# Newton's step of the inverse roots moved to GpSimd, with new places and issue lengths in the plan of the FFN steps

## The chip, the core and the metric

The kernel runs on one core of a Trainium2 chip. The core has five engines with an instruction stream each: TensorE (PE in the profile; its weight loads are shown as PEld), VectorE (DVE), ScalarE (ACT), GpSimd (POOL) and SyncE (SP), which here only issues transfers. Each engine works through its own stream in order and waits at semaphores for the others. The metric is the device time of one execution in microseconds. Every number on the profile comes from one profiled execution.

## The reference

The input is x of shape (8, 512, 128), in float32. Three parts follow one another, each with a residual:

```python
x = x + 0.5 * ffn(layernorm(x))
x = x + latent_attention(layernorm(x))      # 16 heads, causal
x = x + 0.5 * ffn(layernorm(x))             # the same weights as the first

def layer(x):                               # ffn: two of these
    q, k, v = split(shift_token(x) @ wqkv)  # 8 heads of 64
    q = l2norm(q) * q_scale; k = l2norm(k) * k_scale
    q, k = rotary_xpos(q, k)
    p = softmax(mask(8 * q @ k.T))          # windows of 64, each with the one before it
    x = x + (p @ v) @ wo
    h = shift_token(x)
    h = (h - mean(h)) / sqrt(var(h) + 1e-5) * ln_g + ln_b
    a, g = split(h @ w1 + b1)               # 341 columns each
    return x + (a * gelu(g)) @ w2 + b2
```

`shift_token` takes the second half of the 128 channels from the token before. `l2norm` divides each head's 64 values by their norm. So inverse roots are needed in two places: one per token for each layer norm, and one per token, head and side (q or k) for `l2norm`.

## The kernel before

The program has three stages: the FFN part (called f0), the latent attention, and the FFN part again (f1). The FFN stages take two passes (layers) over eight sequences of 512 tokens, so 16 sequences per stage, each in four blocks of 128 tokens. All of X and of the running result Y stays in SBUF.

**Steps.** The function `ffn` doesn't write its instructions directly. It makes *steps* (`step`, line 412): a kind, an engine, a length in us that the plan believes, what is read and written, which buffers are taken, and a function that issues the instructions. The kinds that matter here, with their engine:

- A sequence begins with a norm in the first layer (ist on DVE: statistics; inr on ACT: first guess of the root; ina on DVE: apply), then sh (PE: transposes), sd, sp and sa, which build the shifted transpose hT.
- A block begins with projections qk0, qk1 and v (PE). From each of q and k ACT makes the squares (sq), DVE the two rotary products (cs, lines 543 and 546), and POOL adds them (ad, line 562). ACT copies v out of PSUM (vc), and SP copies it, shifted by 64 tokens, into V2 with two transfers (vd and ve, lines 574 and 580).
- rn (DVE, lines 586 and 589) sums the squares per head. ir (ACT, lines 466 and 467) makes the first guess of the inverse root as exp(-0.5 ln x). nt (DVE, lines 470 to 472) refines it by one step of Newton. km (POOL, line 598) multiplies k by it, and q8 (POOL, line 607) makes 8 times q's root, the scale of the scores.
- tq and tc turn q and k (PE, ACT). sc (PE) makes the scores; mx (DVE, lines 669 and 670) the maxima times q8; ex (ACT, line 677) the exponentials with their sums; rc (DVE) the reciprocals; dv (POOL, line 685) the division. pt (PE) and pc (DVE or ACT, line 723) turn the probabilities; o (PE, line 743) multiplies them with V and V2, oc (ACT) copies, wo (PE) projects, and ya (DVE, line 775) adds into Y.
- After the fourth block the feed-forward part follows: hs (POOL, line 785) copies the unshifted half of Y; hd and he (SP, lines 791 and 798) bring in the other half, shifted by one partition, by transfers. hd covers 127 partitions, he the tokens at the blocks' edges. Then fst (DVE, lines 482 to 484), fnr (ACT) and fna (DVE) normalise in place; b2 (POOL, line 809) adds the bias to Y, which it may only do once hd and he have read Y. Then ft, fc, g, ge, a, u, po (the two products with the gate, line 831 and line 873), y2 and, in the second layer, fi (both DVE) follow. In f1 a transfer fo (SP, line 900) writes the result.

The refinement itself is in `root` (line 462), which returns two functions: `first` for ACT and `newton` for DVE. In the norms `newton` is called at the head of the step "na"; for l2norm it is the step "nt" by itself. An inverse root is refined for 16 numbers per partition in nt and for 4 in a norm. The latent attention has its own `inverse_root` (line 369).

**The plan.** A step's rank is `100 * at + PLACE[kind]` (line 413), where `at` is the number of its block over the whole stage; steps of the start and of the feed-forward part have the number of the sequence's first block. `Plan.run` (line 161) sorts the steps by rank and then plays the stage through: among the first 110 steps still to do (`AHEAD`) it looks which can start when (`ready`, line 122), given the lengths, the buffers, and 0.2 us for a signal between engines. It takes the engine that can begin first and on it the step of lowest rank that can begin within `WHILE` of that time. So PLACE is both a priority on each engine and a limit on how early a step is seen. A step's last number, `after`, is added before others may use its result; for a transfer it stands for the time until it has landed. The order that comes out is fixed in the program: each engine, SP's queue included, runs its instructions in it. The plan's lengths set only the order; on the chip every instruction takes as long as it takes and waits for what it needs.

Of the kernel before, what the change touches and what calls it, by code (L numbers as in the profile page):

```python
# [11 lines left out]
ALU = mybir.AluOpType  # L12
# [8 lines left out]
class PartPool:  # L21
# [7 lines left out]


PLACE = {
    "ist": -350, "inr": -670, "ina": -499, "sh": -750, "sd": -770, "sp": -690, "sa": -560,
    "qk0": -460, "sq0": -600, "cs0": -290, "ad0": -300, "qk1": -350, "sq1": -420, "cs1": -400,
    "ad1": -420, "v": -319, "vc": -89, "vd": -69, "ve": -29, "rn": -118, "ir": -48, "nt": -238,
    "km": -98, "q8": -407, "tq0": -250, "tc0": -600, "tq1": -169, "tc1": -29, "sc": -40,
    "mx": 100, "ex0": 230, "rc0": 90, "dv0": 370, "ex1": 171, "rc1": 131, "dv1": 271, "pt0": 150,
    "pc0": 230, "pt1": -809, "pc1": -909, "o": 190, "oc": 330, "wo": 0, "ya": 70, "hs": 100,
    "hd": 950, "he": 990, "fst": 830, "fnr": 180, "fna": 321, "b2": 500, "ft": 540, "fc": 690,
    "g": 1050, "ge": 1260, "a": 581, "u": 871, "po": 520, "y2": 940, "fi": 790, "fo": 1270,
}  # L40


# [41 lines left out]
class Plan:  # L84
# [5 lines left out]

    SIGNAL = 0.2
    AHEAD = 110
    WHILE = 0.05

    def __init__(self, tc, nc):
        self.tc, self.nc = tc, nc
# [92 lines left out]
def kernel(  # L189
# [219 lines left out]
    def ffn(tagname, last):  # L409
# [52 lines left out]
        def root(x, y, t):  # L462


            def first():
                nc.scalar.activation(y.tile, x.tile, AF.Ln)  # L466
                nc.scalar.activation(y.tile, y.tile, AF.Exp, scale=-0.5)  # L467

            def newton():
                nc.vector.scalar_tensor_tensor(t.tile, y.tile, -0.5, y.tile, ALU.mult, ALU.mult)  # L470
                nc.vector.tensor_mul(t.tile, t.tile, x.tile)
                nc.vector.scalar_tensor_tensor(y.tile, t.tile, 1.5, y.tile, ALU.add, ALU.mult)

            return first, newton

        def norm(k, w, src, dst, reads, writes, slots):

            st, mv, rs, ns, nt = (Slot(r) for r in (r_st, r_mv, r_rs, r_ns, r_nt))

            def stats():  # L480
                for i in range(NB):
                    nc.vector.bn_stats(st[:, i], src()[:, i])
                    nc.vector.bn_aggr(mv[:, i], st[:, i])
                nc.vector.tensor_scalar(rs.tile, mv[:, :, 1], LN_EPS, None, ALU.add)

            first, newton = root(rs, ns, nt)

            def apply():
                newton()
                for i in range(NB):  # L490
                    nc.vector.tensor_scalar(
                        dst()[:, i], src()[:, i], mv[:, i, 0:1], ns[:, i : i + 1],
                        ALU.subtract, ALU.mult,
                    )

            step(w + "st", DVE, 1.6, k, stats, reads, [rs], [st, mv, rs] + slots)
            step(w + "nr", ACT, 0.45, k, first, [rs], [ns], [rs, ns])
            step(w + "na", DVE, 1.7, k, apply, [ns] + reads, writes, [mv, rs, ns, nt] + slots)

        def transposes(src, dst):  # L500
            for i in range(NB):
# [25 lines left out]
        def begin(l, b, i, k):  # L527
            hT, kT, V2, V = seqs[l, b]
            sq, qk = Slot(r_sq), Slot(r_qk)
            x, y, t, q8 = (Slot(r) for r in (r_sums, r_root, r_half, r_q8))  # L530

            def project(ps, at):
                nc.tensor.matmul(  # L533
                    ps.tile, lhsT=hT[:, i * P : (i + 1) * P],
                    rhs=wqkv_sb[l][:, at * INNER : (at + 1) * INNER], start=True, stop=True,
                )

            for s in range(2):
                ps, c1, s1 = Slot(mm), Slot(r_c), Slot(r_s)

                def turned(s=s, ps=ps, c1=c1, s1=s1):
                    psv = ps.tile.rearrange("p (h d) -> p h d", d=DH)
                    nc.vector.tensor_mul(  # L543
                        c1.tile, psv, tabs[l][:, 2 * s, i].unsqueeze(1).to_broadcast([P, H, DH])
                    )
                    nc.vector.tensor_mul(  # L546
                        s1.tile.rearrange("p h (t d) -> p h t d", t=2),
                        psv.rearrange("p h (t d) -> p h t d", t=2)[:, :, ::-1],
                        tabs[l][:, 2 * s + 1, i].rearrange("p (t d) -> p t d", t=2)
                        .unsqueeze(1).to_broadcast([P, H, 2, HD]),  # L550
                    )

                step(f"qk{s}", PE, 0.91, k, lambda s=s, ps=ps: project(ps, s), [hT], [ps], [ps, hT], 0.1)
                step(
                    f"sq{s}", ACT, 0.5, k,
                    lambda s=s, ps=ps: nc.scalar.activation(sq[:, s], ps.tile, AF.Square),  # L556
                    [ps], [sq], [ps, sq], 0.1,
                )
                step(f"cs{s}", DVE, 1.25, k, turned, [ps], [c1], [ps, c1, s1], 0.1)
                step(  # L560
                    f"ad{s}", POOL, 1.28, k,
                    lambda s=s, c1=c1, s1=s1: nc.gpsimd.tensor_add(  # L562
                        qk[:, s].rearrange("p (h d) -> p h d", d=DH), c1.tile, s1.tile
                    ),
                    [c1], [(qk, s)], [c1, s1, qk],
                )
            ps = Slot(mm)
            step("v", PE, 0.95, k, lambda: project(ps, 2), [hT], [ps], [ps, hT], 0.1)
            step(
                "vc", ACT, 0.5, k, lambda: nc.scalar.copy(V[:, i], ps.tile),  # L570
                [ps], [(V, i)], [ps, V], 0.1,
            )
            step(
                "vd", SP, 0.1, k, lambda: nc.sync.dma_start(out=V2[WIN:, i], in_=V[:WIN, i]),
                [(V, i)], [(V2, i)], [V, V2], 3.0,
            )
            if i + 1 < NB:
                step(
                    "ve", SP, 0.1, k,
                    lambda: nc.sync.dma_start(out=V2[:WIN, i + 1], in_=V[WIN:, i]),  # L580
                    [(V, i)], [(V2, i + 1)], [V, V2], 3.0,
                )


            def sums():
                nc.vector.tensor_reduce(
                    x.tile, sq.tile.rearrange("p s (h d) -> p (s h) d", d=DH), AX.X, ALU.add
                )
                nc.vector.tensor_scalar(x.tile, x.tile, 1e-24, None, ALU.max)

            first, newton = root(x, y, t)
            step("rn", DVE, 1.3, k, sums, [sq], [x], [sq, x])
            step("ir", ACT, 0.45, k, first, [x], [y], [x, y])
            step("nt", DVE, 0.55, k, newton, [x, y], [(y, 1)], [x, y, t])

            def scale_k():
                kv = qk[:, 1].rearrange("p (h d) -> p h d", d=DH)
                nc.gpsimd.tensor_mul(  # L598
                    kv, kv, y[:, H:].unsqueeze(2).to_broadcast([P, H, DH])
                )  # L600

            step(
                "km", POOL, 1.05, k, scale_k, [(y, 1), (qk, 1)], [(qk, 2)], [y, qk],
            )
            step(
                "q8", POOL, 0.25, k,
                lambda: nc.gpsimd.tensor_scalar(q8.tile, y[:, :H], 8.0, None, ALU.mult),
                [(y, 1)], [q8], [y, q8],
            )
            blk[l, b, i] = qk, q8  # L610
# [168 lines left out]
        def feed_forward(l, b, k):  # L779
# [4 lines left out]
            def near():  # L784
# [2 lines left out]

            step("hs", POOL, 0.6, k, near, y, [(hs, 0)], [hs])
            step(
                "hd", SP, 0.1, k,  # L790
                lambda: nc.sync.dma_start(
                    out=hs[1:P, :, half:], in_=Y[0 : P - 1, b, :, half:]
                ),
                y, [(hs, 1)], [hs], 3.0,
            )
            step(
                "he", SP, 0.1, k,
                lambda: nc.sync.dma_start(
                    out=hs[0:1, 1:NB, half:], in_=Y[P - 1 : P, b, 0 : NB - 1, half:]
                ),  # L800
                y, [(hs, 2)], [hs], 3.0,
            )
            norm(
                k, "f", lambda: hs, lambda: hs, [(hs, 0), (hs, 1), (hs, 2)], [(hs, 3)], [hs]
# [84 lines left out]
            if l == L - 1:  # L889
                step(  # L890
                    "fi", DVE, 0.65, k,
                    lambda: nc.vector.scalar_tensor_tensor(
                        res.tile if last else X[:, b], Y[:, b], 0.5, X[:, b], ALU.mult, ALU.add
                    ),
                    y, [res if last else ("X", b)], [res] if last else [],
                )
                if last:
                    step(
                        "fo", SP, 0.1, k,
                        lambda: nc.sync.dma_start(  # L900
                            out=out[b].rearrange("(n p) c -> p n c", p=P), in_=res.tile
                        ),
                        [res], [], [res], 3.0,
                    )
# [452 lines left out]
```

## Time and profile before

| what | value |
|---|---|
| median of 3 runs | 2164.95 us (2156.89 to 2168.74) |
| the profiled execution, its own time | 2160.44 us |
| its span on the core | 2158.7 us |
| granted TensorE clock, mean | 0.95 of full speed |
| first stage (f0), from the first norm to the last update of X | 14 to 872 us |
| second FFN stage (f1), from its first statistics to the end | 1308 to 2159 us |
| transfers over the span | 50.01 MB, 23 GB/s |

How to read the profile: the page lists each engine's busy time and its share of the span; the chain that ended last, followed back from the last instruction, each piece put down to the engine or transfer that released the next; and groups of instructions by source line with shape, count, busy time, mean duration, and the idle time ahead of them with what ended it. The trace behind the page answers for single lines, windows and waits. An "L562" is line 562 of the kernel. "SPq" is SP's queue at work on issuing a transfer. Idle time of an engine that is not on the chain costs nothing by itself.

### The profile page before, as it was taken

Reading aid. Unit: us, or ns where it says so; the run is one execution under the profiler, and the core shown is the slowest. Engines: PE = TensorE matmul, PEld = TensorE weight load, DVE = VectorE, ACT = ScalarE, POOL = GpSimd, SP = SyncE. Lnnn points to the kernel's source line nnn. Section 1 sums busy time; section 2 is a strip of 40 time slices with the busy share of each in tenths; the row PEclk is TensorE's granted clock in tenths of the full one; section 3 lists DMA queues with packets and bytes.
Section 4 is the critical chain, followed back from the end, with each engine's and each line's share of the span. In section 5 each row is a group of like instructions: output and inputs, shape, how many; then the busy total and the mean of one; then the engine's idle time right before and its main releaser. Section 6 shows DMA issues by size and latency. Waiting matters only on the chain.

```text
span 2158.7 us, 50620 instructions
## 1 busy us (share of the span) xinstructions
PE 1861.0 (86%) x19860; PEld 1221.2 (57%) x19860; DVE 1556.8 (72%) x3424; ACT 1390.9 (64%) x3921; POOL 847.9 (39%) x969
## 2 busy tenths in 40 slices
PE   3888888999888887699999997888888989888886
PEld 1555555665555565466666653555555555555654
DVE  4997888777777864776665626888888877777854
ACT  2776777777666775135555554877777767666764
POOL 3654445454444541300000003644445544444541
PEclk9999999999999998799999998999999999999998
DMA  4110100010010100000000000100011100111110
GB/s 128 25 27 20 26 21 22 22 23 21 21 24 21 23 21 6 24 12 13 14 14 13 12 3 18 29 20 21 21 25 24 23 21 21 25 26 26 26 28 18
DMA packets 50767, 50.01 MB, mean 23 GB/s; under 512 B 22343, under 2 KB 33329, under 8 KB 50529
## 3 DMA queue, kind: packets, MB, share of 16 engines
q1 hardware_dynamic: 46172, 42.58, 8.5%
q10 hardware_dynamic: 4356, 4.20, 0.6%
q8 instruction: 157, 2.57, 0.5%
q14 instruction: 82, 0.66, 0.1%
HBM read 6.30 MB, written 2.10 MB: 4 GB/s over the span
## 4 chain that ended last, share of the span: by engine, by line
PE 42%; DVE 27%; ACT 9%; DMA 6%; SPq 4%; issue 3%; POOL 1%; ACTq 0%; DVEq 0%; POOLq 0%
DMA hs_f<-Y 5%; PE mm_f L533 5%; PE mm_f L502 5%; PE st L1102 4%; PE mm_f L831 4%; PE lo L1118 4%; DVE c_f L543 4%; ACT pr_f L677 4%; PE sc L1040 4%; PE mm_f L873 4%; DVE s_f L546 4%; PE mm_f L743 3%; SPq L580 3%; ACT sq_f L556 2%; PE st L1095 2%
## 5 line engine op out<-in xcount | busy, mean ns | idle before, releaser
L562 POOL TENSOR_TENSOR qk_f<-c_f,s_f 128x512 f32<-128x512 f32 x256 | 325.4, 1271 | 544.9 <-DVE s_f L546 423.8
L677 ACT ACTIVATE pr_f<-sc_f,nm_f,q_f 128x128 f32<-128x128 f32 x1024 | 456.0, 463 | 50.6 <-DVE nm_f L670 48.7
L533 PE MATMUL mm_f<-wqkv,hT_f 128*128 128x512 f32 x768 | 409.6, 627 | 44.9 <-DVE pT_f L723 20.5
L1109 ACT ACTIVATE pl<-st 128x512 f32<-128x512 f32 x320 | 175.9, 595 | 183.6 <-PE st L1102 111.4
L685 POOL TENSOR_TENSOR pr_f<-pr_f,rso_f 128x512 f32<-128x512 f32 x256 | 266.5, 1051 | 67.8 <-DVE rso_f L701 66.5
L556 ACT ACTIVATE sq_f<-mm_f 128x512 f32<-128x512 f32 x256 | 154.6, 605 | 159.6 <-DVE s_f L546 108.8
L543 DVE TENSOR_TENSOR c_f<-mm_f,tab 128x512 f32<-128x512 f32 x256 | 175.0, 684 | 86.2 <-PE mm_f L533 35.1
L1040 PE MATMUL sc<-k_heads,q_heads 32*128 32x384 f32 (+3 forms) x1024 | 227.4, 468 | 5.1 <-DMA k_heads<-kl 5.1
L502 PE MATMUL mm_f<-ident,qk_f 128*128 128x128 f32 x1024 | 165.4, 288 | 75.7 <-POOL qk_f L598 62.2
L831 PE MATMUL mm_f<-fT_f,w 128*128 128x512 f32 (+1 forms) x384 | 196.7, 623 | 27.4 <-DVE Y L775 14.1
L677 ACT ACTIVATION_READ_ACCUMULATOR pr_f<-sc_f,nm_f,q_f 128x1 f32 x1024 | 214.1, 209 | 0.0
L1102 PE MATMUL st<-q_heads,k_heads 32*128 32x384 f32 (+3 forms) x1024 | 212.9, 435 | 0.0
L743 PEld LDWEIGHTS mm_f<-pT_f,V_f 128*64 128x64 f32 (+1 forms) x4096 | 148.4, 137 | 110.5 <-issue 35.3
L533 PEld LDWEIGHTS mm_f<-wqkv,hT_f 128*128 128x128 f32 x768 | 123.0, 195 | 117.1 <-DVE pT_f L723 48.3
L743 PE MATMUL mm_f<-pT_f,V_f 128*64 128x64 f32 (+1 forms) x4096 | 180.5, 230 | 6.8 <-ACT ns_f L467 3.8
L502 PE MATMUL mm_f<-ident,pr_f 128*128 128x128 f32 x1024 | 155.6, 285 | 33.0 <-ACT ir_f L466 17.2
L502 PEld LDWEIGHTS mm_f<-ident,qk_f 128*128 128x128 f32 x1024 | 118.6, 145 | 113.8 <-POOL qk_f L598 74.5
L1048 DVE TENSOR_REDUCE lnm<-sc 128x1 f32<-128x512 f32 (+1 forms) x192 | 122.2, 685 | 72.1 <-PE sc L1040 50.2
L546 DVE TENSOR_TENSOR s_f<-mm_f,tab 128x512 f32<-128x512 f32 x256 | 173.9, 679 | 0.0
L1152 POOL TENSOR_TENSOR X<-X,lon 128x128 f32<-128x128 f32 x32 | 14.5, 453 | 402.8 <-DVE lon L1148 370.1
L502 PEld LDWEIGHTS mm_f<-ident,pr_f 128*128 128x128 f32 x1024 | 120.3, 145 | 87.8 <-issue 52.6
L767 PEld LDWEIGHTS mm_f<-wo,oT_f 128*128 128x128 f32 x1024 | 142.4, 210 | 47.3 <-ACT oT_f L756 28.4
(143 smaller groups left out, 3822.5 us busy)
## 6 DMA issues: line engine op xcount, KB each, us to landing
V_f<-V_f SPq DMA_DIRECT2D x224, 128.0 KB
hs_f<-Y SPq DMA_DIRECT2D x32, 127.0 KB
X<-in_x_dram SPq DMA_DIRECT2D x8, 256.0 KB
q_heads<-ql SPq DMA_DIRECT2D x64, 32.0 KB
k_heads<-kl SPq DMA_DIRECT2D x64, 32.0 KB
out_dram<-hs_f SPq DMA_DIRECT2D x8, 256.0 KB
wqkv<-in_wqkv_dram ACTq DMA_DIRECT2D x2, 768.0 KB
w<-in_w_dram ACTq DMA_DIRECT2D x2, 341.0 KB
```

Of the source, the lines that this page charges most:

```text
L502: nc.tensor.transpose(dst[:, i * P : (i + 1) * P], src(i), ident)
L533: nc.tensor.matmul(ps.tile, lhsT=hT[:, i * P : (i + 1) * P], rhs=wqkv_sb[l][:, at * INNER : (at + 1) * INNER], start=True, stop=True,)
L543: nc.vector.tensor_mul(c1.tile, psv, tabs[l][:, 2 * s, i].unsqueeze(1).to_broadcast([P, H, DH]))
L546: nc.vector.tensor_mul(s1.tile.rearrange("p h (t d) -> p h t d", t=2), psv.rearrange("p h (t d) -> p h t d", t=2)[:, :, ::-1], tabs[l][:, ...
L556: lambda s=s, ps=ps: nc.scalar.activation(sq[:, s], ps.tile, AF.Square),
L562: lambda s=s, c1=c1, s1=s1: nc.gpsimd.tensor_add(qk[:, s].rearrange("p (h d) -> p h d", d=DH), c1.tile, s1.tile),
L677: nc.scalar.activation(pr[:, h], sv[:, h % 2, h // 2], AF.Exp, bias=nm[:, h % 2, h // 2 : h // 2 + 1], scale=q8[:, h : h + 1], accum_out=s ...
L685: nc.gpsimd.tensor_mul(pr[:, heads], pr[:, heads], inv[:, heads].unsqueeze(2).to_broadcast([P, H // 2, P]),)
L743: nc.tensor.matmul(o[r * DH : (r + 1) * DH, u * P + w * WIN : u * P + (w + 1) * WIN], lhsT=(V2, V)[w][keys, i, h * DH : (h + 1) * DH], rhs ...
L831: nc.tensor.matmul(ps[: hsz[c], :], lhsT=w1_sb[l][:, at + c * P : at + c * P + hsz[c]], rhs=fT.tile, start=True, stop=True,)
L1040: yield lambda i=i, j=j, at=at, n=n: nc.tensor.matmul(bank[:, at : at + (i + 1) * P], lhsT=qp[rows, j, i * P : (i + 1) * P], rhs=kp[rows, ...
L1102: yield lambda c=c, j=j, at=at, n=n: nc.tensor.matmul(bank[:, at : at + T - c * P], lhsT=kp[rows, j, c * P : (c + 1) * P], rhs=qp[rows, j, ...
```

## The change

Four things change, all in the FFN stages.

1. `newton` is issued on POOL, with four instructions in place of three.
2. In a norm it becomes a step of its own, "nn", between "nr" and "na"; "nt" moves from DVE to POOL. The lengths in the plan follow: na 1.7 to 1.15, nn 0.9, nt 0.55 to 0.95.
3. The plan's lengths of the transfers' issues grow (vd and ve 0.1 to 0.6, hd, he and fo 0.1 to 0.8), and the times to landing of vd, ve, hd and he shrink (3.0 to 2.2 or 2.6). `WHILE` goes from 0.05 to 0.
4. All numbers of PLACE are new, so the order of every engine's work in these stages can be another.

The arithmetic of the root is the same: y (1.5 - 0.5 x y y). The latent attention keeps its code.

```diff
 PLACE = {
-    "ist": -350, "inr": -670, "ina": -499, "sh": -750, "sd": -770, "sp": -690, "sa": -560,
-    "qk0": -460, "sq0": -600, "cs0": -290, "ad0": -300, "qk1": -350, "sq1": -420, "cs1": -400,
-    "ad1": -420, "v": -319, "vc": -89, "vd": -69, "ve": -29, "rn": -118, "ir": -48, "nt": -238,
-    "km": -98, "q8": -407, "tq0": -250, "tc0": -600, "tq1": -169, "tc1": -29, "sc": -40,
-    "mx": 100, "ex0": 230, "rc0": 90, "dv0": 370, "ex1": 171, "rc1": 131, "dv1": 271, "pt0": 150,
-    "pc0": 230, "pt1": -809, "pc1": -909, "o": 190, "oc": 330, "wo": 0, "ya": 70, "hs": 100,
-    "hd": 950, "he": 990, "fst": 830, "fnr": 180, "fna": 321, "b2": 500, "ft": 540, "fc": 690,
-    "g": 1050, "ge": 1260, "a": 581, "u": 871, "po": 520, "y2": 940, "fi": 790, "fo": 1270,
+    "ist": -500, "inr": -780, "inn": -420, "ina": -889, "sh": -460, "sd": -490, "sp": -510,
+    "sa": -550, "qk0": -370, "sq0": -420, "cs0": -280, "ad0": -390, "qk1": -350, "sq1": -530,
+    "cs1": -470, "ad1": -330, "v": -249, "vc": -169, "vd": -69, "ve": -279, "rn": -488,
+    "ir": -338, "nt": -168, "km": -408, "q8": -387, "tq0": -440, "tc0": -370, "tq1": -239,
+    "tc1": -549, "sc": -90, "mx": -600, "ex0": -230, "rc0": 80, "dv0": 40, "ex1": 11, "rc1": -49,
+    "dv1": -9, "pt0": 200, "pc0": -40, "pt1": -139, "pc1": -409, "o": 50, "oc": -220, "wo": 380,
+    "ya": 120, "hs": 360, "hd": 540, "he": 550, "fst": 720, "fnr": 490, "fnn": 420, "fna": 381,
+    "b2": 410, "ft": 90, "fc": 30, "g": 1000, "ge": 920, "a": 421, "u": 71, "po": 700, "y2": 500,
+    "fi": 1070, "fo": 430,
 }
...
-    WHILE = 0.05
+    WHILE = 0.0
...
             def newton():
-                nc.vector.scalar_tensor_tensor(t.tile, y.tile, -0.5, y.tile, ALU.mult, ALU.mult)
-                nc.vector.tensor_mul(t.tile, t.tile, x.tile)
-                nc.vector.scalar_tensor_tensor(y.tile, t.tile, 1.5, y.tile, ALU.add, ALU.mult)
+                nc.gpsimd.tensor_mul(t.tile, y.tile, y.tile)
+                nc.gpsimd.tensor_mul(t.tile, t.tile, x.tile)
+                nc.gpsimd.tensor_scalar(t.tile, t.tile, -0.5, 1.5, ALU.mult, ALU.add)
+                nc.gpsimd.tensor_mul(y.tile, y.tile, t.tile)
...
             def apply():
-                newton()
                 for i in range(NB):
...
-            step(w + "na", DVE, 1.7, k, apply, [ns] + reads, writes, [mv, rs, ns, nt] + slots)
+            step(w + "nn", POOL, 0.9, k, newton, [rs, ns], [(ns, 1)], [rs, ns, nt])
+            step(w + "na", DVE, 1.15, k, apply, [(ns, 1)] + reads, writes, [mv, ns] + slots)
...
-                "vd", SP, 0.1, k, lambda: nc.sync.dma_start(out=V2[WIN:, i], in_=V[:WIN, i]),
-                [(V, i)], [(V2, i)], [V, V2], 3.0,
+                "vd", SP, 0.6, k, lambda: nc.sync.dma_start(out=V2[WIN:, i], in_=V[:WIN, i]),
+                [(V, i)], [(V2, i)], [V, V2], 2.2,
...
-                    "ve", SP, 0.1, k,
+                    "ve", SP, 0.6, k,
...
-                    [(V, i)], [(V2, i + 1)], [V, V2], 3.0,
+                    [(V, i)], [(V2, i + 1)], [V, V2], 2.2,
...
-            step("nt", DVE, 0.55, k, newton, [x, y], [(y, 1)], [x, y, t])
+            step("nt", POOL, 0.95, k, newton, [x, y], [(y, 1)], [x, y, t])
...
-                "hd", SP, 0.1, k,
+                "hd", SP, 0.8, k,
...
-                y, [(hs, 1)], [hs], 3.0,
+                y, [(hs, 1)], [hs], 2.6,
...
-                "he", SP, 0.1, k,
+                "he", SP, 0.8, k,
...
-                y, [(hs, 2)], [hs], 3.0,
+                y, [(hs, 2)], [hs], 2.6,
...
-                        "fo", SP, 0.1, k,
+                        "fo", SP, 0.8, k,
```

## The prediction

> **What bounds the kernel now.** I read the page first: shares of busy time and the chain that ended last.
>
> ```profile
> span 2158.7 us, 50620 instructions
> PE 1861.0 (86%) x19860; PEld 1221.2 (57%) x19860; DVE 1556.8 (72%) x3424; ACT 1390.9 (64%) x3921; POOL 847.9 (39%) x969
> PE 42%; DVE 27%; ACT 9%; DMA 6%; SPq 4%; issue 3%; POOL 1%; ACTq 0%; DVEq 0%; POOLq 0%
> ```
>
> PE is busiest, yet it holds the chain for only 42% of the span. DVE holds it for 27%, transfers and SP's queue for 10%. The two FFN stages (until about 872 us, and from 1308 us on) are where the diff acts; the latent attention between them (436 us) is untouched. I then laid two windows over one sequence (four blocks) each. The columns are the stretch, its length, then the busy time of PE, PEld, DVE, ACT, POOL, then clock and DMA.
>
> ```profile
> 391.00:439.00 48.00, 42.85 (x436) 28.14 (x434) 38.57 (x82) 36.20 (x108) 24.71 (x29) 1.00 0.10 24
> 596.00:648.00 52.00, 45.51 (x436) 29.76 (x436) 39.62 (x89) 36.27 (x109) 25.70 (x28) 0.93 0.09 22
> ```
>
> Same work, two paces. From one start of L809 to the next the f0 stage takes 47.2 to 49.2 us per sequence between 295 and 489 us, and 52.5 to 54.7 us between 489 and 701 us; f1 repeats it. PE's steps run back to back would take less: from chain pieces, a projection 0.86, four transposes 0.44, scores 1.28, values 1.08 (2.1 in the first block of a sequence), the wo product 0.91. That is 31.5 us for four blocks, and 8.7 for shift and feed-forward: an estimate of 40.2 us. So 8 to 14 us per sequence are order and stalls. The groups by line (count, busy us, mean ns, idle before) show one source:
>
> ```profile
> L471 DVE TENSOR_TENSOR irt_f<-irt_f,rn_f 128x16 f32<-128x16 f32 x128 | 53.1, 415 | 4.4
> L472 DVE SCALAR_TENSOR_TENSOR ns_f<-nt_f,ns_f 128x4 f32<-128x4 f32 x48 | 37.7, 785 | 1.6
> L598 POOL TENSOR_TENSOR qk_f<-qk_f,ir_f 128x512 f32<-128x512 f32 x128 | 133.6, 1043 | 9.2
> L607 POOL TENSOR_SCALAR q_f<-ir_f 128x8 f32<-128x8 f32 x128 | 29.8, 233 | 77.8 <-DVE ir_f L472 66.4 <-DVE rso_f L701 6.3 <-DVE nt_f L470 0.7
> L1152 POOL TENSOR_TENSOR X<-X,lon 128x128 f32<-128x128 f32 x32 | 14.5, 453 | 402.8 <-DVE lon L1148 370.1 <-DVE lnm L1055 32.7
> ```
>
> Four or sixteen numbers per partition take 0.4 to 0.8 us. One line's own spread (min/median/max ns) and the timeline say why:
>
> ```profile
> L471 DVE TENSOR_TENSOR irt_f<-irt_f,rn_f x128: 157/175/1265, 48.5 to 2089.0; 128x16 f32<-128x16 f32 x128
> L471 DVE TENSOR_TENSOR nt_f<-nt_f,rs_f x48: 161/1082/1274, 30.3 to 2139.8; 128x4 f32<-128x4 f32 x48
> ```
> ```profile
> 422.84 1.27 POOL L562 TENSOR_TENSOR qk_f<-c_f,s_f 128x512 f32<-128x512 f32 x1 [2.15 <-DVE irt_f L470]
> 423.00 1.14 DVE L472 SCALAR_TENSOR_TENSOR ir_f<-irt_f,ir_f 128x16 f32<-128x16 f32 x1
> ```
>
> The DVE instruction ends when POOL's does. Last, the waits and the transfer in front of the feed-forward norm:
>
> ```profile
> DVE st_f L482 <- DMA hs_f<-Y: 100.0, 21, 7.1
> POOL Y L809 <- DMA hs_f<-Y: 118.7, 22, 9.0
> ```
> ```profile
> 586.23 0.76 SPq L791 DMA_DIRECT2D hs_f<-Y  x1
> 587.04 6.45 SPq L580 DMA_DIRECT2D V_f<-V_f  x1
> 593.54 0.73 SPq L798 DMA_DIRECT2D hs_f<-Y  x1
> 595.46 0.30 DVE L482 BATCH_NORM_STATS2 st_f<-hs_f 128x6 f32<-128x128 f32 x1 [4.15 <-DMA hs_f<-Y]
> ```
> ```profile
> 843.32 0.71 SPq L791 DMA_DIRECT2D hs_f<-Y  x1
> 844.08 6.44 SPq L798 DMA_DIRECT2D hs_f<-Y  x1
> 852.52 0.29 DVE L482 BATCH_NORM_STATS2 st_f<-hs_f 128x6 f32<-128x128 f32 x1 [7.02 <-DMA hs_f<-Y]
> ```
>
> Whatever SP issues behind hd stands 6.4 us, and st can begin 9.2 us after hd's issue. In the slow pace DVE sits 4.2 us before st; in the quick one hd was issued 20 us ahead and nothing waits.
>
> **What the Trainium skill says.** "SBUF — State Buffer", section "SBUF: two separate sides": the port pair that DVE and GpSimd share is an exclusive lock, held for a whole instruction, and a DVE instruction with two SBUF inputs needs it. The trace agrees: 157 ns free, 1265 ns at most, about one 1271 ns L562. "DMA: Bandwidth & Descriptors", section "Why a DMA increments its semaphore by 16 and not by 1": a transfer over 127 partitions is given one DMA engine, where 128 get sixteen. hd covers 127; its 9.2 us fit, though the trace here doesn't count its engines.
>
> **The change, part by part.**
>
> *Newton leaves DVE.* Removed: L470, L471, L472 in 128 nt and 48 na steps: 35.0+53.1+49.7+10.5+35.3+37.7 = 221.3 us of DVE. Their medians when free are about 0.17, so 528 x 0.17 = 90 us is work and 131 us lock. Over the chain's pieces in order of time these lines have 129.2 us (79.5 in 71 ir roots, 49.7 in 27 norms).
>
> *Newton arrives on POOL.* Four instructions, never run there at this size. From L1152 (128 elements, 453 ns) and L598 (512, 1043 ns): 1.54 ns per element and 256 ns fixed. So a tensor_mul takes 0.28 us at 16 elements and 0.26 at 4; the tensor_scalar 0.233 as L607. nt: 3 x 0.28 + 0.23 = 1.07; nn: 1.02; POOL gets 128 x 1.07 + 48 x 1.02 = 186 us, 848 to 1034. Between 60 and 860 us it is busy 389.6 of 800 us; 93 more make 60%: not a bound. If each cost half (0.14) or double, POOL would get 93 or 370 us; I take 186.
>
> What this brings on the chain: where the next piece is a DVE instruction that doesn't read the root, the full piece. Of the 71 ir roots 46 are followed by L723 or L775, which don't: 46/71 x 79.5 = 51 us. Where the root itself is awaited the path becomes ACT, POOL, then q8 and km on POOL without a hop, about 1.2 us against 1.12: 25 x 0.08 = 2 us lost. In the 27 norms L491 follows, which reads it: 49.7 against 27 x 1.3 = 35 gains 15 us if nothing else fills DVE's time, all 50 if cs or rn of another block does; the middle is 33. All 71 roots awaited, and nothing to fill the norms, gives 9 us; everything hidden gives 129. I take 51 - 2 + 33, or 82 us; **85** in round numbers.
>
> *The wait that this adds.* nt now stands in POOL's line until ACT's ir; behind it are ad, dv, q8, km, and for them wait PE's transposes (tq0, tq1, pt). On DVE, na waits for POOL; behind it are cs, mx, rn. Both are hidden if the order leaves room; POOL idles over 40% of the stage.
>
> *Other lock holders.* rn's L589 (322 ns against 174 free), nm L670 (227 against 170) and L491 lose about 35 us to POOL today. With POOL's share up from 49 to 60% that is some 8 us more, **5** of them on the chain.
>
> *Issue lengths.* vd and ve 0.1 to 0.6 (0.46 and 0.59 measured), hd and he 0.1 to 0.8 (0.755 and 0.748): no instruction changes, only the plan's picture. It still lands hd with he at 0.8+0.8+2.6 = 4.2 us, where the trace shows 9.2: 5 us are unplanned.
>
> *Places.* hd moves from 950 to 540, he from 990 to 550, fst from 830 to 720, b2 from 500 to 410. A hundred is one block, 13.1 us in the slow pace. There Y was ready at 561.85 (POOL's copy into hs), hd left 24 us later: with 110 steps in view and about 43 steps per block it was not yet seen. 410 earlier is 54 us, more than 24, so hd leaves when Y is ready, he directly behind it, and both land by 571. st, ready on DVE at 591.3, moves up by 110, 14 us, to 577: 6 us after landing. So the wait of the middle sequences (about 16 x 4.2 = 70 of the 100 us; the rest is drain) should go. But every other place moves too: mx by -700, rn -370, tc1 -520, u -800, wo +380, and the view is filled otherwise. I take half, **35 us**; ends: all 70, or 11 sequences without a wait now get 5 us each, a loss of 55. For the moved POOL order with b2 I charge **10 us**. mx ahead of all DVE work lets ACT's exponentials start sooner; I give nothing for it, since I did not work the whole order out: -60 to +60.
>
> *Sum.* 2160.4 (the profiled run; span 2158.7) - 85 - 35 + 5 + 10 = 2055. The median of the runs is 4.5 us above the profiled run: **2060 us**. Each FFN stage would then take about 802 us, 50 per sequence with ramp and drain (1709 for both now, less 105), well above 40.2.
>
> **Rivals.**
> *Only the latency moves.* The roots are awaited, not DVE's time: 9 to 45 us gained, transfers as now, 2120 to 2150, about 2135. For it: q8 waits 66.4 us for L472 today. Against: DVE's 27% of the chain, mostly of back-to-back work.
> *POOL's line stands behind b2* (slower). b2, now ahead of st in place (410 against 720), is put at the planned landing, 5 us before the real one, with the Newtons of the next blocks behind it; DVE and PE then wait for q8, km and nm. The 21 sequences with a wait pay already; 11 more pay 5.0 us = 55, Newton gains only its 9: 2160 + 46, with the 4.5: about 2210. It decides once Newton's gain is under 55 us. For it: b2 already stands 118.7 us. Against: by the places b2 comes near 578, after 571.
> *The lock follows.* More, shorter POOL instructions catch rn, nm and the applies, and what DVE sheds comes back: the 8 us would have to be tenfold; then no change, 2165.
>
> **How the numbers follow.** A measurement here tells about 0.5%, 11 us, from no change (three runs span 12). Forecast, 1985 to 2115: 0.52. Latency only, 2115 to 2154: 0.16. No change: 0.06. Slower, by b2's mechanism or by an order that fits worse: 0.26, half of it above 2195. Faster thus 0.68. Under 1985 I leave some 5%, above 2190 some 15%. The forecast's own range is 1985 to 2115.
>
> **What would show it.** DVE with 528 instructions fewer and near 1340 us busy; POOL with 704 more and near 1034; new POOL rows of 0.23 to 0.28 us; DVE's wait for hs_f under 65 us; periods between L809 starts of 45 to 49 us throughout. Wrong if POOL's rows cost 0.5, if waits of DVE or PE on POOL's roots pass 100 us, or if st and b2 still wait 5 us in each sequence.

## The result and the profile after

The changed kernel takes 2142.86 us (median of four runs, 2138.77 to 2144.88) against 2165.03 us for the kernel before: a ratio of 0.990, with a 95% interval of 0.987 to 0.993. It is faster by 22 us. The forecast was 105 us, 2060 us. The sign was right; four fifths of the gain didn't come.

First the page of the changed kernel: its span, the busy shares, and the chain that ended last, by engine.

```profile
span 2136.9 us, 50948 instructions
PE 1856.1 (87%) x19860; PEld 1213.7 (57%) x19860; DVE 1374.7 (64%) x2896; ACT 1394.4 (65%) x3921; POOL 994.3 (47%) x1673
PE 50%; DVE 17%; DMA 14%; POOL 7%; ACT 6%; issue 4%; SPq 0%; ACTq 0%; POOLq 0%; DVEq 0%
```

DVE lost the 528 instructions and 182 us of busy time (1556.8 to 1374.7), POOL got 704 instructions and 146 us (847.9 to 994.3). DVE's share of the chain fell from 27% to 17%. But transfers and SP's queue together rose from 10% to 14% of the chain, and the span is only 22 us shorter. The waits of the changed kernel, longest first (engine and line waiting, what for, us in total, times, longest):

```profile
POOL Y L811 <- DMA hs_f<-Y: 170.3, 32, 9.0
DVE st_f L484 <- DMA hs_f<-Y: 151.1, 32, 9.3
PEld mm_f L535 <- POOL nt_f L472: 142.9, 26, 6.0
PE mm_f L535 <- POOL nt_f L472: 137.4, 26, 5.8
```

Before, DVE stood 100.0 us in 21 sequences for hs_f; now 151.1 us in all 32. PE stands 26 times, 5.3 us each. The last two lines name POOL's Newton instruction, which would suggest that the root now comes late. One sequence in the timeline of the changed kernel tells otherwise (start, length, engine and line; in brackets the idle time ahead):

```profile
427.22 0.29 DVE L777 TENSOR_TENSOR Y<-Y,mm_f 128x128 f32<-128x128 f32 x1 [2.76 <-PE mm_f L769]
428.09 0.76 SPq L793 DMA_DIRECT2D hs_f<-Y  x1
428.90 6.59 SPq L800 DMA_DIRECT2D hs_f<-Y  x1
437.45 0.29 DVE L484 BATCH_NORM_STATS2 st_f<-hs_f 128x6 f32<-128x128 f32 x1 [5.00 <-DMA hs_f<-Y]
437.70 1.26 POOL L811 TENSOR_TENSOR Y<-Y,b 128x512 f32<-128x512 f32 x1 [5.63 <-DMA hs_f<-Y]
```

hd leaves as soon as Y is complete, as forecast (within 0.6 us in all 32 sequences). he stands 6.59 us behind it, and the statistics begin 9.36 us after hd's issue, as in the drain of the kernel before. But DVE and POOL are already standing there. ACT follows, then PE, here one sequence earlier:

```profile
389.52 0.20 ACT L467 ACTIVATE ns_f<-rs_f 128x4 f32<-128x4 f32 x1 [5.06 <-DVE rs_f L486]
389.76 0.20 ACT L468 ACTIVATE ns_f<-ns_f 128x4 f32<-128x4 f32 x1
389.87 0.57 ACT L630 COPY qT_f<-mm_f 128x512 f32<-128x512 f32 x1
390.58 3.75 PE L535 MATMUL mm_f<-wqkv,hT_f 128*128 128x512 f32 x4 [5.08 <-POOL nt_f L472]
```

The first guess of the norm's root (L467) holds ACT's line for 5.06 us, because it waits for the statistics. Behind it stands a copy out of PSUM (L630), and PE's next projection starts 0.14 us after that copy ends at 390.44. The copy empties one of the four PSUM banks of the "mm" ring, from which the projection takes its own. That PE waited for this bank is read from the times, not from a record. The POOL instruction named as releaser would then only be the last event before; an experiment below bears this out.

From one start of the bias addition (L811) to the next, sequences take 49.8 to 51.5 us until the drain: the quick pace (47 to 49) and the slow one (52 to 55) of before have become one between them.

The rows of Newton's step in the changed kernel:

```profile
L471 POOL TENSOR_TENSOR irt_f<-ir_f 128x16 f32<-128x16 f32 x128 | 27.5, 215 | 58.7 <-DVE hs_f L492 55.6 <-ACT ir_f L468 3.1
L472 POOL TENSOR_TENSOR irt_f<-irt_f,rn_f 128x16 f32<-128x16 f32 x128 | 29.0, 227 | 10.1
L473 POOL TENSOR_SCALAR nt_f<-nt_f 128x4 f32<-128x4 f32 x48 | 9.5, 199 | 4.2
```

They take 0.20 to 0.23 us each; nt sums to 0.87 us and nn to 0.81.

### The profile page after: what moved, and what is told of

Read it like the earlier page. It is cut to its first block, busy times and chain, and to the rows that moved or that the text cites. A ratio compares the mean times of both kernels' runs of the same rounds, so it can differ in the third digit from the quotient of the medians.

```text
span 2136.9 us, 50948 instructions
## 1 busy us (share of the span) xinstructions
PE 1856.1 (87%) x19860; PEld 1213.7 (57%) x19860; DVE 1374.7 (64%) x2896; ACT 1394.4 (65%) x3921; POOL 994.3 (47%) x1673
## 4 chain that ended last, share of the span: by engine, by line
PE 50%; DVE 17%; DMA 14%; POOL 7%; ACT 6%; issue 4%; SPq 0%; ACTq 0%; POOLq 0%; DVEq 0%
DMA hs_f<-Y 13%; PE mm_f L535 10%; PE mm_f L504 6%; PE mm_f L833 5%; PE st L1104 4%; PE lo L1120 4%; PE mm_f L745 4%; PE sc L1042 4%; PE mm_f L875 3%; PE mm_f L769 3%; DVE c_f L545 3%; DVE rn_f L588 2%; POOL qk_f L564 2%; DVE s_f L548 2%; PE st L1097 2%
## 5 line engine op out<-in xcount | busy, mean ns | idle before, releaser
L535 PE MATMUL mm_f<-wqkv,hT_f 128*128 128x512 f32 x768 | 442.4, 684 | 149.8 <-POOL nt_f L472 137.4
L564 POOL TENSOR_TENSOR qk_f<-c_f,s_f 128x512 f32<-128x512 f32 x256 | 324.5, 1270 | 216.7 <-DVE s_f L548 209.5
L535 PEld LDWEIGHTS mm_f<-wqkv,hT_f 128*128 128x128 f32 x768 | 138.7, 212 | 237.4 <-POOL nt_f L472 142.9
L558 ACT ACTIVATE sq_f<-mm_f 128x512 f32<-128x512 f32 x256 | 150.3, 598 | 107.3 <-DVE s_f L548 94.4
L833 PE MATMUL mm_f<-fT_f,w 128*128 128x512 f32 (+1 forms) x384 | 185.0, 605 | 7.0 <-DVE Y L777 5.2
L504 PE MATMUL mm_f<-ident,qk_f 128*128 128x128 f32 x1024 | 157.0, 281 | 19.7 <-ACT fT_f L821 9.3
L504 PEld LDWEIGHTS mm_f<-ident,qk_f 128*128 128x128 f32 x1024 | 113.5, 141 | 102.6 <-issue 62.5
L588 DVE TENSOR_REDUCE rn_f<-sq_f 128x16 f32<-128x1024 f32 x128 | 155.0, 1211 | 25.8 <-ACT sq_f L558 25.4
L671 DVE TENSOR_REDUCE nm_f<-sc_f 128x8 f32<-128x1024 f32 x128 | 155.6, 1216 | 19.0 <-PE sc_f L662 18.7
```

Source lines behind the costliest of these rows:

```text
L504: nc.tensor.transpose(dst[:, i * P : (i + 1) * P], src(i), ident)
L535: nc.tensor.matmul(ps.tile, lhsT=hT[:, i * P : (i + 1) * P], rhs=wqkv_sb[l][:, at * INNER : (at + 1) * INNER], start=True, stop=True,)
L564: lambda s=s, c1=c1, s1=s1: nc.gpsimd.tensor_add(qk[:, s].rearrange("p (h d) -> p h d", d=DH), c1.tile, s1.tile),
L588: nc.vector.tensor_reduce(x.tile, sq.tile.rearrange("p s (h d) -> p (s h) d", d=DH), AX.X, ALU.add)
L833: nc.tensor.matmul(ps[: hsz[c], :], lhsT=w1_sb[l][:, at + c * P : at + c * P + hsz[c]], rhs=fT.tile, start=True, stop=True,)
```

## The experiments

Two theories stood after the result. **T1**: the transfer in front of the feed-forward norm ate the gain. The plan believes that hd and he have landed 4.2 us after hd's issue, so it puts the statistics, b2 and the first guess there; in truth it takes over 9 us, and every engine stands the difference out. **T2**: Newton's step on POOL is worth little, because the roots are awaited; the transfer only fills time in which something else would be missing.

All times below are medians, and each ratio is to the kernel before run on the same chip alongside. The new `WHILE` and the single places were not tried by themselves.

### The transfer made quick, in the order of the changed kernel and of the one before

```diff
-                lambda: nc.sync.dma_start(
-                    out=hs[1:P, :, half:], in_=Y[0 : P - 1, b, :, half:]
-                ),
+                lambda: [
+                    nc.sync.dma_start(
+                        out=hs[lo + 1 : hi + 1, :, half:], in_=Y[lo:hi, b, :, half:]
+                    )
+                    for lo, hi in ((0, 112), (112, P - 1))
+                ],
```

The plan's lengths are left alone, so PE, DVE, ACT and POOL keep the order of their instructions; SP issues one transfer more per sequence.

> The changed kernel with hd issued as two transfers, of 112 and of 15 partitions, in place of one of 127; the order of all steps stays. Theory T1 (the transfer in front of the feed-forward norm ate the gain): hd and he land some 3 us after the issue instead of 8.5 to 9.2, so the 151 us that DVE stands before the statistics and the 137 us that PE stands beside it nearly all go; 32 sequences by 3.5 to 4.5 us, 110 to 145 us: 2000 to 2030 us. Theory T2 (the roots now come late from GpSimd, as the wait of PE on the nt_f tile suggests): the transfer was only another engine's idle time; gain under 40 us, 2105 to 2140 us, and PE still waits over 100 us on GpSimd's root.

Measured: 1982.72 us, ratio 0.916 (0.914 to 0.917). That is 160 us less than the changed kernel. The page and the waits for hs_f of this kernel:

```profile
PE 1805.5 (91%) x19860; PEld 1195.9 (60%) x19860; DVE 1376.6 (70%) x2896; ACT 1393.5 (70%) x3921; POOL 994.7 (50%) x1673
PE 53%; DVE 29%; ACT 9%; issue 4%; POOL 3%; DMA 1%; SPq 0%; ACTq 0%; DVEq 0%; POOLq 0%
```
```profile
POOL Y L814 <- DMA hs_f<-Y: 6.1, 2, 3.1
DVE st_f L484 <- DMA hs_f<-Y: 6.0, 2, 3.0
```

Transfers fall from 14% of the chain to 1%, DVE's wait from 151.1 to 6.0 us, and PE's 137.4 us "for POOL's nt_f" to 6.8, with POOL's Newton unchanged. T1 holds, T2's reading of that wait falls. The gain is above T1's 110 to 145.

> The kernel before with hd issued as two transfers of 112 and 15 partitions; order as before. T1: DVE's wait of 100 us goes, and the 6.4 us that SP stands behind hd; but 11 of 32 sequences had no wait, so the gain is smaller than in the changed kernel: 60 to 95 us, 2070 to 2105 us, and all sequences take 48 to 49 us. T2 says nothing else here.

Measured: 2072.92 us, ratio 0.957 (0.956 to 0.959): 90 us, as T1 had it. The sequences take 48 to 51 us throughout, except the first and the drain. So the slow transfer cost the kernel before 90 us and the changed one 160.

### Is it the partitions, or the dividing?

```diff
-                    for lo, hi in ((0, 112), (112, P - 1))
+                    for lo, hi in ((0, 113), (113, P - 1))
```

> The changed kernel with hd in two transfers of 113 and 14 partitions; 113 is a prime number like 127. If a transfer over a prime number of partitions goes through one DMA engine, the first one still lands about 8 us after its issue and stops SP's next issue for some 5.5 us: no gain, 2125 to 2155 us. If it is the dividing by itself that helps (two transfers in flight), most of the 160 us of the 112 and 15 division come: 1985 to 2040 us.

Measured: 2122.76 us, ratio 0.982 (0.980 to 0.984): 20 us better than one transfer (just under the 2125 to 2155 expected), and 140 us behind the division into 112 and 15. In the timeline of this kernel SP still stands behind the first part (both parts as one row), and DVE waits:

```profile
429.09 6.52 SPq L794 DMA_DIRECT2D hs_f<-Y  x2
435.66 0.72 SPq L803 DMA_DIRECT2D hs_f<-Y  x1
437.71 0.29 DVE L484 BATCH_NORM_STATS2 st_f<-hs_f 128x6 f32<-128x128 f32 x1 [3.75 <-DMA hs_f<-Y]
```

The statistics begin 8.62 us after the first issue, against 9.36. With 112 partitions both parts are issued in 1.64 us, and where DVE does stand waiting, in the last sequence of a stage, the statistics begin 2.95 us after the first issue:

```profile
762.48 1.59 SPq L794 DMA_DIRECT2D hs_f<-Y  x2
765.43 0.29 DVE L484 BATCH_NORM_STATS2 st_f<-hs_f 128x6 f32<-128x128 f32 x1 [3.02 <-DMA hs_f<-Y]
```

The number of partitions decides, not the dividing. The rule that the prediction took from the Trainium skill ("DMA: Bandwidth & Descriptors", section "Why a DMA increments its semaphore by 16 and not by 1": the largest number up to 16 that divides the partitions, so 1 for 127 and 113, and 16 for 112) fits all three. The trace doesn't name the engines, but it has their mean busy share. Stretches while the first part is under way, in the changed kernel, with 113 and with 112 partitions (the last two columns are the busy share of the sixteen DMA engines and GB/s):

```profile
432.00:433.00 1.00, 1.00 (x36) 0.81 (x32) 0.45 (x1) 1.00 (x4) 0.06 (x1) 1.00 0.08 18
433.00:434.00 1.00, 1.00 (x22) 0.57 (x24) 0.97 (x2) 1.00 (x5) 0.52 (x2) 1.00 0.08 18
447.00:447.50 0.50, 0.50 (x17) 0.50 (x18) 0.50 (x2) 0.50 (x3) 0.37 (x2) 1.00 0.80 165
```

A share of 0.08 is 1.3 engines of sixteen, so about one; 0.80 is 13. An estimate from these figures: hd's 127 KB at 18 GB/s take 7.2 us, most of the 9.36.

### The plan told the truth, the transfer left slow

```diff
-                "he", SP, 0.8, k,
+                "he", SP, 6.5, k,
...
-                y, [(hs, 2)], [hs], 2.6,
+                y, [(hs, 2)], [hs], 2.0,
```

> The changed kernel, one transfer of 127 partitions as before, but the plan is told what the trace shows: he takes 6.5 us to issue and lands 2.0 us later (in place of 0.8 and 2.6). Places unchanged. T1: the plan now puts other work ahead of the statistics and of b2 while the transfer is under way; DVE's wait of 151 us falls under 60 and the time to 2030 to 2090 us. Rival: with the places unchanged the longer chain only moves the wait (ACT's or PE's), 2110 to 2160 us.

Measured: 1995.84 us, ratio 0.923 (0.921 to 0.924): 147 us better than the changed kernel, more than T1 expected, by two numbers that only the planner reads. SP's order is the same; the other engines' differs. In its timeline the transfer is as slow as ever, and DVE arrives just as it lands:

```profile
442.99 0.76 SPq L793 DMA_DIRECT2D hs_f<-Y  x1
443.80 6.44 SPq L800 DMA_DIRECT2D hs_f<-Y  x1
452.18 0.29 DVE L484 BATCH_NORM_STATS2 st_f<-hs_f 128x6 f32<-128x128 f32 x1 [0.35 <-DMA hs_f<-Y]
```

DVE's wait for hs_f is 17.9 us in all, over 27 times. POOL's b2 still waits 60.5 us; as the whole kernel is within 13 us of the one with the quick transfer, that can't cost much. Its chain is a warning:

```profile
PE 49%; DVE 22%; DMA 13%; POOL 8%; ACT 4%; issue 3%; SPq 0%; ACTq 0%; POOLq 0%; DVEq 0%
```

Transfers hold 13% of it, nearly the 14% of the changed kernel. The chain still runs through the transfer, but the other engines have work in the meantime. So the share of the chain didn't show what the transfer cost; the experiments did.

> The kernel before (old places, Newton on VectorE, one transfer of 127 partitions) with only the plan told the truth on hd and he: issues of 0.8 and 6.5 us, he landed 2.0 later. T1: DVE's wait of 100 us goes as with the two transfers, 2070 to 2110 us. Rival: hd and he have places (950, 990) behind the statistics (830), so the wait stays and only moves, 2140 to 2175 us.

Measured: 2140.84 us, ratio 0.991 (0.989 to 0.994), at the edge of the rival's range. T1 missed this one: 22 us, where the quick transfer in the unchanged order gave 90. DVE's wait for hs_f did go, against the rival's reason (14.0 us are left, 4 times), but the order that the old places give with these lengths has other waits in its stead: PE's weight loads of the wo product wait 73.4 us for ACT's copy L756 (28.4 before), POOL's additions 94.1 us for the reciprocals L701 (9.0 before). Nor was the plan told the whole truth here. In 18 of the 32 sequences this order has ve directly behind hd; there ve stands 6.5 us, not he, and the plan still believes in 0.1 for it. So the two numbers that gave 147 us with the new places gave 22 with the old ones; what wholly true lengths would give there wasn't tried.

### The lengths alone

The changed kernel with the old lengths of the transfers: 0.1 for each issue and 3.0 to landing.

```diff
-                "hd", SP, 0.8, k,
+                "hd", SP, 0.1, k,
...
-                "he", SP, 0.8, k,
+                "he", SP, 0.1, k,
...
-                y, [(hs, 2)], [hs], 2.6,
+                y, [(hs, 2)], [hs], 3.0,
```

(vd, ve and fo likewise.)

> The changed kernel with the old lengths of the transfers in the plan (issues 0.1, landing 3.0); new places and Newton on GpSimd as changed, one transfer of 127 partitions. If the new lengths matter because they widen what the plan leaves for hd and he (from 3.2 to 4.2 us, of 9 real), about 1 us more per sequence now: 2155 to 2180 us. If they don't matter beside the places: 2135 to 2150 us.

Measured: 2214.06 us, ratio 1.024 (1.022 to 1.026): slower than before, 71 us slower than the changed kernel, and beyond both expectations. The waits of this kernel for hs_f:

```profile
DVE st_f L484 <- DMA hs_f<-Y: 206.2, 32, 7.3
POOL Y L811 <- DMA hs_f<-Y: 176.8, 32, 9.0
```

Here the plan leaves 3.2 us for hd and he. The kernels with the new places and Newton on POOL, set in a row (from the first issue to the start of the statistics, median of the sequences; for 112 and 15 of the two that waited):

| kernel | time for hd and he, plan | in truth | DVE's wait for hs_f | time |
|---|---|---|---|---|
| old lengths | 3.2 us | 9.3 us | 206.2 us | 2214.06 us |
| the changed kernel | 4.2 us | 9.3 us | 151.1 us | 2142.86 us |
| 113 and 14 partitions | 4.2 us | 8.7 us | 131.0 us | 2122.76 us |
| plan told of 6.5 us | 9.3 us | 9.3 us | 17.9 us | 1995.84 us |
| 112 and 15 partitions | 4.2 us | 3.0 us | 6.0 us | 1982.72 us |

From end to end that is 1.16 us of time for each us of DVE's wait (231 over 200.2 us), and between 1.0 and 1.3 from row to row. The first and the fourth kernel have an order of their own, so not all of their difference need be the wait; the other three have the same order on PE, DVE, ACT and POOL.

### Lengths that fit the quick transfer

> The changed kernel with hd in two transfers (112 and 15 partitions) and the plan told so: hd 1.6 us to issue, he 0.8, landing 2.0 us after. The lengths in the plan then fit the trace and no wait is left to remove (DVE stood 6 us in all for hs_f without this): 1970 to 1990 us, the same as without the new lengths (1983 us). A gain of over 15 us would mean that other steps were still late.

Measured: 1981.14 us, ratio 0.916 (0.915 to 0.918), the same as with the changed kernel's lengths. No wait was left to remove.

### Newton's part, alone and undone

Newton back on VectorE in the changed kernel (its steps and lengths as before):

```diff
-            step("nt", POOL, 0.95, k, newton, [x, y], [(y, 1)], [x, y, t])
+            step("nt", DVE, 0.55, k, newton, [x, y], [(y, 1)], [x, y, t])
```

and the norms' "nn" taken back into "na".

> The changed kernel with Newton's step back on VectorE (three instructions; nt 0.55 on VectorE, na 1.7 as before), all else as changed. T1: DVE's 220 us return, but part of them falls into the 5 us per sequence in which everything stands anyway: 20 to 70 us slower than the changed kernel, 2165 to 2215 us. T2: no slower than the changed kernel, 2120 to 2145 us.

Measured: 2160.11 us, ratio 0.9986 (0.997 to 1.000). Places and lengths without Newton's move are worth 3 us, hardly clear of the noise; the move adds 17. T2 is refuted (it said no slower), T1's lower end (2165) missed by 5 us.

Newton alone on POOL, places and lengths as before, with places for the new kind ("inn" -500, "fnn" 320):

> The kernel before with only Newton's step on GpSimd (nn at places -500 and 320, between its neighbours); places, issue lengths and the choice of steps as before. T1: Newton by itself is worth the 60 to 85 us that the chain of before suggested, where the transfer doesn't wait: 2080 to 2110 us. T2: within 15 us of before, 2150 to 2180 us.

Measured: 2117.95 us, ratio 0.978 (0.976 to 0.980): 45 us, between the theories. Part of it is the transfer again: in this order DVE stands 65.6 us for hs_f, in 16 sequences, in place of 100.0 in 21.

The same two with the quick transfer (112 and 15):

> The changed kernel with hd in two transfers (112 and 15 partitions) and Newton's step back on VectorE: new places and lengths without the wait and without Newton's move. T1: the transfer's wait was worth some 140 us here too, so 2020 to 2060 us; the difference to the same kernel with Newton on GpSimd (1983 us) is what Newton is worth once the wait is gone: 40 to 75 us. T2 (Newton on GpSimd buys little wherever it stands): at most 2000 us.

Measured: 2015.69 us, ratio 0.932 (0.930 to 0.934). T2 fails; T1's range (2020 to 2060) is missed by 4 us. Newton's move is worth 33 us here (2015.69 to 1982.72), somewhat under the 40 to 75 named.

> The kernel before with hd in two transfers and only Newton's step on GpSimd; places and lengths as before. If the parts simply add (two transfers 90 us, Newton 45 us): 2028 us. If the new places are worth something only once the transfer doesn't stand in the way: about 2020 to 2035 us, 40 to 50 us above the 1983 us that they reach with both. If the places are worth nothing at all: about 1985 us.

Measured: 2047.45 us, ratio 0.947 (0.946 to 0.949). This is above all three expectations, 65 us above the kernel with the new places and lengths (1982.72), and 25 below the same without Newton's move (2072.92). The parts don't add. All eight together, in us:

| | transfer of 127 | 112 and 15 |
|---|---|---|
| before | 2163 | 2073 |
| Newton on POOL alone | 2118 | 2047 |
| places and lengths alone | 2160 | 2016 |
| both (the change) | 2143 | 1983 |

On the left the places and lengths are worth 3 us or cost 25; on the right they gain 57 or 65. Newton's move gains 17 to 45 us in every pair.

### What the move of Newton costs by itself

Two kernels in the order of the kernel before. In one, Newton's four POOL instructions stand where the three of DVE stood, and the plan isn't told. In the other the step is left out.

```diff
             def newton():
-                nc.vector.scalar_tensor_tensor(t.tile, y.tile, -0.5, y.tile, ALU.mult, ALU.mult)
-                nc.vector.tensor_mul(t.tile, t.tile, x.tile)
-                nc.vector.scalar_tensor_tensor(y.tile, t.tile, 1.5, y.tile, ALU.add, ALU.mult)
+                pass
```

> The kernel before with the four instructions of Newton's step on GpSimd, issued where the three stood, and nothing else: the plan is left with its old picture, so every other instruction keeps its place on its engine. If the move itself is worth what the chain of before shows (85 us as forecast, between 9 and 129): about 2080 us. If the roots are mostly awaited, on whichever engine: 2140 to 2175 us, and the 45 us of the kernel with Newton alone came from the plan's new order.

Measured: 2158.97 us, ratio 0.997 (0.996 to 0.998): 4 us. Waits of this kernel: POOL now stands for ACT's first guess of the root, and PE longer for km, which comes behind it on POOL.

```profile
POOL irt_f L470 <- ACT ir_f L467: 121.1, 74, 3.2
DVE st_f L483 <- DMA hs_f<-Y: 121.1, 21, 7.5
PE mm_f L503 <- POOL qk_f L599: 88.3, 40, 6.7
```

Before, PE's wait for km was this:

```profile
PE mm_f L502 <- POOL qk_f L598: 62.2, 16, 6.1
```

> The kernel before without Newton's step in the FFN stages (left out of the computation: the inverse roots stay the first guess by exp and ln); order of all the rest unchanged. This is the most that any move of Newton can bring here. If the 129 us that the chain of before has in Newton's lines were all gain: 2035 us. If other work moves into its place on the chain: 2080 to 2110 us.

Measured: 2085.76 us, ratio 0.964 (0.962 to 0.966): 77 us. So the 129 us that Newton's lines had on the chain were worth 77 when they vanish, and 4 when they move in an order that wasn't made for it. The 45 us of Newton alone needed the new order that the plan made with it.

## Why the prediction was wrong, and where it was right

Of the forecast's terms, Newton was booked at 80 us (85, less 5 for the lock) and the places at 25 (35, less 10 for b2). In the order of the changed kernel they came as 17 and 3.

**The transfer: the failed step of the places.** "410 earlier is 54 us ... st, ready on DVE at 591.3, moves up by 110, 14 us, to 577: 6 us after landing. So the wait of the middle sequences ... should go." It treated a place as an offset in time on the chip. hd and he did leave when Y was ready. But a place only makes a step visible and ranks it; when the plan starts st depends on when the plan believes hd and he to have landed. With hd early enough, it put st right there in every sequence, some 5 us too soon. What was booked as a gain of 35 us became a wait of 151.1 us in 32 sequences in place of 100.0 in 21. The loss named as the other end, "11 sequences without a wait now get 5 us each", was what happened to DVE: +51 us.

**The lengths: the term booked at nothing.** "no instruction changes, only the plan's picture." The sentence that followed had the key: "5 us are unplanned". Only the loss end and the slower rival made use of it; the sum has nothing for it. With the new places the new lengths, which widen the gap by 1 us, are worth 71 us (vd, ve and fo included), and the 5 us that they still lack 147.

**Newton: it leaves DVE as forecast, but brings far less.** DVE's busy time fell by 182 us of the 221 removed. Part of the rest is the rival "the lock follows": L486, a tensor_scalar of four numbers, rose from 353 to 691 ns and now stands against L564 (1.03 us at 388.46), and L492 over Y rose from 467 to 591 ns. POOL's price was overestimated: 0.87 and 0.81 us for 1.07 and 1.02. The gain of 85 us was oversized: taking the step away altogether gives 77 in the old order, and moving it gave 4, 17, 25, 33 or 45 depending on the order around it. Two steps are at fault. "the next piece is a DVE instruction that doesn't read the root, the full piece" looked one piece ahead; 129 us on the chain were worth 77, so other work took the place. And "the wait that this adds" was booked at nothing because POOL idles over 40% of the stage. In the old order the move brings 4 of the 77 that leaving the step out brings: POOL stands 121.1 us for ACT's first guess, and PE's wait for km behind it rises from 62.2 to 88.3 us.

**The rivals.** The slower rival put the stall into POOL's line, with Newton behind b2. b2 does stand 170.3 us; but in the kernel told of 6.5 us it still stands 60.5 us at little cost, and in the timeline the stall goes from the statistics over ACT's first guess to PE. The two waits have the same cause and were never parted, so b2's share stays open. "by the places b2 comes near 578, after 571" failed as st's did. "Only the latency moves" foresaw a time of 2135, near the measured one, partly by luck: its 9 to 45 us for Newton hold the 17, but it took the transfers to stay as they were, and without their wait the whole change is worth 90 us (2072.92 to 1982.72).

**What was right.** The counts of instructions, POOL not a bound (47% of the span), hd leaving with Y, and the reason for the long transfer, which the division into 112 and 15 turned into 160 us. One of the prediction's own signs of being wrong came true: st and b2 wait about 5 us in each sequence.

## What to carry to other kernels

Where an order is fixed from believed durations, a wrong duration of one transfer can be paid in every round: here 151.1 us on DVE and 137.4 on PE, with no engine but PE over 65% busy. Compare each believed landing with the trace before retuning anything else, and shorten the transfer or correct the number; correcting alone gave 147 us with one set of places and 22 with the other. A wait's named releaser may only be the last event; test the suspects by an edit that leaves one of them as it is. The share of a line on the chain was not what its move brought (129 us on the chain, 77 gone with the step, 4 to 45 with its move), and a retuned order couldn't be judged from its numbers alone.

## What the runs showed of the hardware

**A gap on PE costs more than its length.** The changed kernel in stretches of 5 us around one stall (length, busy time of PE, PEld, DVE, ACT, POOL with counts, granted clock, DMA):

```profile
381.00:386.00 5.00, 4.50 (x58) 3.21 (x57) 1.29 (x2) 3.41 (x10) 0.94 (x2) 1.00 0.09 22
386.00:391.00 5.00, 0.42 (x1) 0.45 (x2) 4.06 (x12) 1.44 (x5) 3.19 (x6) 0.72 0.24 54
391.00:396.00 5.00, 5.00 (x41) 2.10 (x41) 4.22 (x11) 2.86 (x12) 2.37 (x8) 0.59 0.00 0
396.00:401.00 5.00, 4.71 (x57) 3.65 (x57) 4.50 (x12) 4.55 (x15) 3.16 (x4) 1.00 0.01 3
```

With the 5 us of standing, the mean granted clock of a stretch fell to 0.72 and then 0.59 before it returned to 1.00, and the first two projections (four matmul rows) took 3.75 us, where the same four rows took 1.98 at 379.87. The line's spread says the same: 593 ns in the median, 1220 at most. The Trainium skill has this in "TensorE: Matmul & The Clock Gate", section "Part 1: The HAM clock gate": a window of some 3.4 us without work halves PE's clock until it has been busy for such a window again. The trace agrees. The prediction had not counted it, and priced waits at their length alone. How much it is can be read from PE: its 19860 instructions took 1856.1 us in the changed kernel and 1805.5 with 112 and 15 partitions, 51 us less for the same work, 48 of them in the projections (442.4 against 394.7 us). The mean clock of the whole run follows: 0.932 with the old lengths, 0.941 in the changed kernel, 0.977 with 112 and 15 partitions, 0.982 with the plan told of 6.5 us. This may be why a microsecond of DVE's wait was worth more than one of time; it wasn't tested by itself.

**127 or 113 partitions against 112.** Behind one transfer of 127 partitions SP's next issue took 6.4 to 6.6 us; with 113 up to 5.7; with 112 neither of the two issues behind it took over 1.8.
